# Transposing the attention probabilities of the first pair of heads with VectorE and DMAs in place of TensorE

## The chip, the cores and the metric

The kernel runs on one core of one Trainium2 chip. The core has five engines that run their own instruction streams in order: TensorE (PE in the profile; its weight loads are the row PEld), VectorE (DVE), ScalarE (ACT), GpSimd (POOL) and SyncE (SP), which here only issues DMAs. They meet by semaphores. The metric is the device time of one execution in microseconds (us). Three runs of the kernel before took 1125.55, 1126.14 and 1126.27 us; the median, 1126.14 us, is the time before. Everything is float32.

## The reference

Three layers are applied in turn to x, which is 4 batches x 256 tokens x 512: a layer of gated experts, causal attention with 32 heads, and the experts again. Each takes a layernorm of x as its input and adds to x.

```python
def _L0_attn_ref(hidden_states, wq, wkv, wo):
    q = jnp.einsum('bsd,de->bse', hidden_states, wq).reshape(B, S, H, DQ)
    kv = jnp.einsum('bsd,de->bse', hidden_states, wkv)
    k = kv[..., :H * DN].reshape(B, S, H, DN)
    v = kv[..., H * DN:H * (DN + DV)].reshape(B, S, H, DV)
    scores = jnp.einsum('bqhd,bkhd->bhqk', q[..., :DN], k) * scale
    scores = jnp.where(causal[None, None], scores, NEG_INF)
    probs = jax.nn.softmax(scores, axis=-1)
    attn = jnp.einsum('bhqk,bkhd->bqhd', probs, v).reshape(B, S, H * DV)
    return jnp.einsum('bse,ed->bsd', attn, wo)
...
x = x + 0.5 * _L0_ffn_ref(_layernorm(x, axis=-1), L0_ffn_A, L0_ffn_B, L0_ffn_Wr)
x = x + _L0_attn_ref(_layernorm(x, axis=-1), L0_attn_wq, L0_attn_wkv, L0_attn_wo)
x = x + 0.5 * _L0_ffn_ref(_layernorm(x, axis=-1), L0_ffn_A, L0_ffn_B, L0_ffn_Wr)
```

In the attention H is 32 heads, B 4 batches, S 256 tokens and DN = DV = 128. Of the 256 x 256 probabilities of a head and a batch only the causal part is computed: for the first 128 queries 128 keys, for the other 128 queries 256 keys. That is a tile of 128 partitions (queries) by 384 columns. To multiply it with the values, TensorE needs it with the keys on the partitions, so it has to be transposed in three blocks of 128 x 128.

## The kernel before, in words

**Pairs and units.** The heads are worked off in 16 pairs (NG = 16, index p). A pair has eight units, one for each head and batch (`units`, in the order head, then batch). A unit passes through `probs` (L1170): two kinds of score matmuls into one PSUM tile `ps` (L1178, L1179, 0.65 us of TensorE), the masked and scaled copy with the row minimum on VectorE (L1187, two parts), the exponential with the row sum on ScalarE (L1199, two parts), the reciprocal of the sums on VectorE (L1208), and then the division by the sum and the transposition, for which there are two ways.

- The classic way (`by_dma` false): ScalarE multiplies in place (L1212, two parts); later `turn` (L1236) has TensorE transpose the three blocks into PSUM (L1241, tile `ptp`), and ScalarE copies them to `pT` (L1245).
- The other way: ScalarE writes the multiplied probabilities to a PSUM tile `pn` in a permuted order (L1217, two parts), VectorE transposes it in blocks of 32 x 32 back into `s` (L1223, one instruction of 128 x 384), four DMAs on SP's queue bring the blocks to the tile `moved` in DRAM (L1226, 48 KB each), and one more brings `moved` to `pT` (L1232, 192 KB). TensorE has no part in it.

`probs` is a generator: each `yield` ends a piece, and `take(made, n)` issues the next n pieces. `attend` (L1247) then multiplies `pT` with the values (L1255, L1262, tile `pa`) and has ScalarE copy the result to `attn` (L1269). `pT` has two buffers, `s` and `moved` three, and the PSUM pool of `pn`, `ptp` and `pa` two.

**Which units take which way.** `classic(number)` says it: before the change the first eight units (pair 0) and the last ten are classic, the 110 between go the other way. In the middle pairs the products of a unit come 17.5 us of written time after its scores (`PRODUCT`), about three units later, and the DMA to `pT` is issued 10.8 us after them (`BACK`).

**What else runs.** Beside the units TensorE computes the queries and keys of the next pair (`make_qk`, tiles `pqk_a` to `pqk_e`, L730) and the values (`make_v`, tiles `pv_a` to `pv_e`, L829). Each stage takes seven products by Strassen's scheme; VectorE adds each product from PSUM to the results (L747 for `qk`, L854 for `vbuf`), ScalarE copies some (L754, L779, L860, L884), and GpSimd forms sums of weights (L611) and a few sums of results (L781, L886). A later product of a stage goes into the PSUM bank of an earlier one, so it waits until that one was read. The pool of these banks has five.

**What sets the order.** In pair 0 only TensorE's order is written out: `FIRST_UNITS` has one string for each unit, in which f, g, q and v take the next product of a stream of queries and keys or of values, t is a `turn` and b an `attend`, both of the unit before. The orders of the other engines and of SP's queue in pair 0 are made by a planner, which goes by the program's order and by costs that it assumes. From pair 1 on all five orders are written out, by a clock of assumed costs: `later(time, what, ...)` puts an event (`turn_at`, `attend_at`, `take`) at a time, and the products of queries, keys and values fill the rest (`goes_on`). The last pieces of pair 0, the `turn` and the `attend` of unit 7, are such events in pair 1.

Of the kernel before, what the change touches and what calls it, by code (L numbers as in the profile page):

```python
# [22 lines left out]
NG = H // HG  # L23
# [10 lines left out]
def macaron_kernel(  # L34
# [173 lines left out]
    def take(steps, n):  # L208
        for _ in range(n):
            next(steps, None)  # L210
# [421 lines left out]
    def begin_qk(p):  # L632

        weights["qk", p] = two_levels(
            qkpool,
            7,
            f"wqk_{p}",
            lambda k, n: [view[:, 2 * k : 2 * k + 2, p * HG + n, 0:DN] for view in (wq_v, wk_v)],
        )
# [530 lines left out]
    def probs(h, b, by_dma=True):  # L1170


        n = f"{h}_{b}"
        p, j = divmod(h, HG)
        half, a = divmod(b, 2)
        qT, kT = (qks[p][:, BLOCK[half][j], i, a * S : (a + 1) * S] for i in range(2))
        ps = ps_s.tile([P, 512], F32, tag="s", name=f"ps_{n}")
        nc.tensor.matmul(ps[:, 0:P], lhsT=qT[:, 0:P], rhs=kT[:, 0:P], start=True, stop=True)  # L1178
        nc.tensor.matmul(ps[:, P : 3 * P], lhsT=qT[:, P : 2 * P], rhs=kT, start=True, stop=True)  # L1179

        s = work.tile([P, 3 * P], F32, tag="s", name=f"s_{n}", bufs=3)
        least = small.tile([P, 2], F32, tag="least", name=f"least_{n}")
        den = small.tile([P, 2], F32, tag="aden", name=f"aden_{n}")
        rden = small.tile([P, 2], F32, tag="arden", name=f"arden_{n}")
        parts = (slice(0, P), slice(P, 3 * P))
        for i, cols in enumerate(parts):
            nc.vector.tensor_tensor_reduce(  # L1187
                out=s[:, cols],
                in0=ps[:, cols],
                in1=mask_f[:, cols],  # L1190
                scale=-SCALE,
                scalar=-TAKEN,
                op0=ALU.add,
                op1=ALU.min,
                accum_out=least[:, i : i + 1],
            )
        yield
        for i, cols in enumerate(parts):
            nc.scalar.activation(  # L1199
                s[:, cols],  # L1200
                s[:, cols],
                AF.Exp,
                bias=least[:, i : i + 1],
                scale=-1.0,
                accum_out=den[:, i : i + 1],
            )
        yield
        nc.vector.reciprocal(rden, den)  # L1208
        yield
        if not by_dma:  # L1210
            for i, cols in enumerate(parts):
                nc.scalar.mul(s[:, cols], s[:, cols], rden[:, i : i + 1])  # L1212
            pTs[h, b] = s
            return
        pn = ps_t.tile([P, 4, 3, 32], F32, tag="pt", name=f"pn_{n}")
        for i, cols in enumerate(parts):
            nc.scalar.mul(  # L1217
                pn[:, :, i : 2 * i + 1, :].rearrange("p k t c -> p t k c"),
                s[:, cols].rearrange("p (t k c) -> p t k c", k=4, c=32),
                rden[:, i : i + 1],  # L1220
            )
        yield
        nc.vector.transpose(s, pn.rearrange("p k t c -> p (k t c)"))  # L1223
        moved = turning.tile([P, 4, 96], F32, tag="moved", name=f"moved_{n}")
        for q in range(4):
            nc.sync.dma_start(  # L1226
                moved[:, q].rearrange("(k r) x -> r k x", r=32),
                s[32 * q : 32 * q + 32].rearrange("r (k x) -> r k x", k=4),
            )
        yield  # L1230
        pT = pTs[h, b] = work.tile([P, 4, 3, 32], F32, tag="pT", name=f"pT_{n}")
        nc.sync.dma_start(pT.rearrange("p q t c -> p (q t c)"), moved.rearrange("p q x -> p (q x)"))  # L1232
# [3 lines left out]
    def turn(h, b):  # L1236

        s = pTs[h, b]
        pt = ps_t.tile([P, 3, 4, 32], F32, tag="pt", name=f"ptp_{h}_{b}")
        for i in range(3):  # L1240
            nc.tensor.transpose(  # L1241
                pt[:, i].rearrange("p q c -> p (q c)"), s[:, i * P : (i + 1) * P], ident
            )
        pT = pTs[h, b] = work.tile([P, 4, 3, 32], F32, tag="pT", name=f"pT_{h}_{b}")
        nc.scalar.copy(pT.rearrange("p q t c -> p t q c"), pt)  # L1245
# [101 lines left out]
    units = [(h, b) for h in range(H) for b in range(B)]  # L1347
# [31 lines left out]
    def later(time, what, *of):  # L1379
        heapq.heappush(events, (time, len(events) + 1000 * len(order), what, of))  # L1380
        order.append(None)
# [18 lines left out]

    def classic(number):

        return number < 8 or number >= 8 * NG - 10


    EXP, PART, MUL, TURN, BACK, PRODUCT = 2.1, 3.5, 4.3, 6.0, 10.8, 17.5
# [56 lines left out]
    for p in range(NG):  # L1463
        last = p == NG - 1
        streams = {"q": make_qk(p + 1), "v": make_v(p), "f": first_qk, "g": first_v}
        if p == NG - 2:
            streams_o = out_products()
        if p == 0:
            for unit in range(HG * B):
                made = probs(*units[unit], False)  # L1470
                for _ in made:
                    pass
                for k in FIRST_UNITS[unit]:
                    if k in "tb":
                        if unit:
                            (turn if k == "t" else attend)(*units[unit - 1])
                    else:
                        take(streams[k], 1)
            for k in "fgqv":
                take(streams[k], 100)  # L1480
            written_out.close()
            written_out.enter_context(tc.manual_schedule(engines=ENGINES))
            rights[0][0]()
            later(1.0, turn_at, *units[7])
            later(2.2, attend_at, *units[7])
            continue
        if last:

            xscope.close()
            streaming = ExitStack()  # L1490
            stream["pool"] = streaming.enter_context(
                tc.tile_pool(name="stream", bufs=3, reuse_waits="tile")
            )
            streams["o"] = streams_o
            outer["rest"]()
            outer["load"](1)
            parts = [[("o", 0.44)] * n for n in (6, 6, 6, 5, 5, 5, 6, 6)]
        else:
            steps = merged(p)
            share = sum(cost for _, cost in steps) / 8  # L1500
            parts, t = [[] for _ in range(8)], 0.0
            for step in steps:
                parts[min(7, int((t + 0.5 * step[1]) / share))].append(step)
                t += step[1]
        for unit in range(HG * B):
            if unit == 2:
                lefts[p - 1] = left_sums_of(p - 1)

            def transfers(p=p, unit=unit):

                if p < NG - 2:
                    if unit == min(Q_LOADS):
                        begin_qk(p + 2)
                    for m in Q_LOADS.get(unit, ()):
                        weights["qk", p + 2][1](m)
                k = p // 2 + 1
                if p % 2 == 0 and 2 * k < NG:
                    if unit == min(V_LOADS):
                        begin_v(k)
                        v_by[k] = v_stages(k)  # L1520
                    for m in V_LOADS.get(unit, ()):
                        weights["v", k][1](m)
                for back in (1, 2):
                    if p - back >= 0 and not (p == NG - 1 and back == 1):
                        stores = LEFT_STORES[2 if p - back == NG - 3 else (p - back + 1) % 2].get(unit + 8 * (back - 1), ())
                        for parts in stores:
                            lefts[p - back][1](parts)
                if p == NG - 1:
                    last_transfers(unit)
                    return  # L1530
                if unit == 3:
                    rights[p - 1][2]()
                if unit == (3 if p == NG - 2 else 7):
                    rights[p][0]()
                if p == NG - 2:
                    if unit in (5, 6):
                        take(streams_o, 1)

            if p == NG - 1 and unit == 3:
                for one in lefts[p - 1][0]:  # L1540
                    one()
            written(p, unit, parts[unit], streams, transfers)
        for k in "qv":
            take(streams[k], 100)
# [87 lines left out]
```

## Time and profile before

One profiled execution took 1124.15 us, 1.99 us less than the median of the runs; its span (first to last instruction) is 1122.3 us, and 1.85 us lie around it. The rows used here:

| what | value |
|---|---|
| median of three runs | 1126.14 us (1125.55 to 1126.27) |
| profiled execution, span | 1124.15 us, 1122.3 us |
| TensorE, granted clock | 1.00 |
| stage of the change: scores of unit 0 to scores of unit 8 | 148.1 to 212.1 us of the span |
| first scores of units 1 to 7 | 152.7, 167.4, 175.6, 180.3, 188.3, 198.8, 207.3 us |
| products of units 0 to 7 | 159.5, 171.9, 178.3, 184.2, 193.2, 203.2, 210.6, 215.5 us |
| three transposes on TensorE (L1241) | 0.33 us from their start to the next matmul |
| copy of the transposed blocks (L1245) | 0.48 us |
| transposition on VectorE (L1223) | 0.577 us |

Times of single instructions are given as start and duration in us, counted from the start of the span. Matmuls overlap: an instruction's duration is longer than the time until the next one starts, and that time is what it costs TensorE. "Idle before" names the instruction that ended the wait, as the program that makes the profile infers it from semaphores. The row PEld counts the weight loads that each matmul needs.

### The profile page before, as it was taken

What the parts mean: (1) busy time and instruction counts of PE and PEld (TensorE: products, weight loads), DVE (VectorE), ACT (ScalarE), POOL (GpSimd) and SP (SyncE); (2) the same over time, 40 slices, a digit from 0 to 9 for tenths busy, and PEclk for the clock granted to TensorE, in tenths of its full rate; (3) what the DMA queues carried; (4) which work ended last, traced back from release to release, by engine and by line L of the source; (5) the groups of instructions that cost most, each with busy time, mean ns of one, the idle gap of its engine ahead of it and who ended that gap; (6) DMA issues with size and microseconds to landing.
All of it is one profiled execution on the core that took longest, in us unless ns stands there. A gap on an engine that the chain in (4) does not pass through costs nothing.

```text
span 1122.3 us, 21075 instructions
## 1 busy us (share of the span) xinstructions
PE 1110.7 (99%) x6834; PEld 977.4 (87%) x6834; DVE 807.3 (72%) x2234; ACT 441.9 (39%) x1328; POOL 626.5 (56%) x870
## 2 busy tenths in 40 slices
PE   9999999999999999999999999999999999999998
PEld 6666888899999999999999998999899999995767
DVE  5554677778778778778778778868778977865432
ACT  4453424444544544544544544544452000107310
POOL 4814487737887887887888788878532000002110
PEclk9999999999999999999999999999999999999999
DMA  9201020156756746746756756655799998750001
GB/s 332 86 1 38 29 67 16 31 145 197 203 138 195 210 136 193 207 136 192 203 152 174 210 144 183 190 166 161 205 311 321 335 348 264 243 180 1 19 19 38
DMA packets 198013, 180.06 MB, mean 160 GB/s; under 512 B 73488, under 2 KB 161296, under 8 KB 197648
## 3 DMA queue, kind: packets, MB, share of 16 engines
q1 hardware_dynamic: 197904, 178.72, 52.5%
q8 instruction: 55, 0.90, 0.3%
q14 instruction: 54, 0.44, 0.1%
HBM read 112.98 MB, written 65.67 MB: 159 GB/s over the span
## 4 chain that ended last, share of the span: by engine, by line
PE 90%; DMA 3%; DVE 2%; POOL 2%; SPq 1%; ACT 1%; issue 1%; POOLq 0%; DVEq 0%
PE po_M L1154 15%; PE po_f L422 9%; PE pqk_c L730 8%; PE ph_f L354 8%; PE pqk_b L730 8%; PE pqk_d L730 7%; PE pa L1255 5%; PE pv_c L829 4%; PE ps L1179 4%; PE pqk_a L730 3%; PE pv_b L829 3%; PE pa L1262 2%; PE ps L1178 2%; PE pv_d L829 2%; PE pv_e L829 2%; PE pv_a L829 2%
## 5 line engine op out<-in xcount | busy, mean ns | idle before, releaser
L384 POOL TENSOR_TENSOR hg_f<-hg_f,gate_f 128x512 f32<-128x512 f32 x32 | 33.5, 1059 | 259.5 <-ACT gate_f L309 151.1
L1154 PE MATMUL po_M<-or_M,ol_M 128*128 128x128 f32 x1456 | 164.7, 275 | 0.0
L1154 PEld LDWEIGHTS po_M<-or_M,ol_M 128*128 128x128 f32 x1456 | 163.7, 192 | 0.1
L611 POOL TENSOR_TENSOR wqk_M<-wqk_M 128x128 f32<-128x128 f32 x320 | 141.7, 458 | 12.1
L747 DVE TENSOR_TENSOR qk<-qk,pqk_d 128x512 f32<-128x512 f32 x210 | 116.6, 561 | 18.9 <-PE pqk_d L730 13.1
L611 POOL TENSOR_TENSOR wqk_M<-wqk_M,wqk_M 128x512 f32<-128x512 f32 (+1 forms) x64 | 107.2, 1683 | 38.7 <-DMA wqk_M<-in_wkv 23.0
L1199 ACT ACTIVATE s<-s,least 128x128 f32<-128x128 f32 (+1 forms) x256 | 114.3, 450 | 21.1 <-DVE least L1187 20.9
L1217 ACT ACTIVATE pn<-s,arden 128x128 f32<-128x128 f32 x220 | 93.7, 426 | 54.4 <-DVE arden L1208 50.7
L730 PE MATMUL pqk_c<-xop,wqk_M 128*128 128x256 f32 x448 | 111.3, 380 | 0.1
L730 PE MATMUL pqk_d<-xop,wqk_M 128*128 128x256 f32 x420 | 106.8, 381 | 1.1 <-DVE qk L747 1.1
L730 PE MATMUL pqk_b<-xop,wqk_M 128*128 128x256 f32 x420 | 104.0, 380 | 0.0
L747 DVE TENSOR_TENSOR qk<-qk,pqk_c 128x256 f32<-128x256 f32 (+1 forms) x112 | 59.7, 533 | 52.2 <-PE pqk_c L730 50.9
L1269 ACT COPY attn<-pa 128x256 f32<-128x256 f32 x128 | 47.4, 371 | 124.4 <-PE pa L1262 121.7
L1054 DVE TENSOR_TENSOR ol_M<-ol_M 128x512 f32<-128x512 f32 x104 | 75.1, 722 | 23.0 <-DMA ol_M<-left 22.6
L747 DVE TENSOR_TENSOR qk<-qk,pqk_b 128x512 f32<-128x512 f32 x105 | 71.7, 683 | 26.7 <-PE pqk_b L730 25.1
L730 PEld LDWEIGHTS pqk_c<-xop,wqk_M 128*128 128x128 f32 x448 | 78.7, 191 | 8.4 <-ACT qk L779 1.2
L1187 DVE CUSTOM_DVE_ANT_0 s<-ps,mask 128x128 f32<-128x128 f32 (+1 forms) x256 | 80.8, 353 | 3.8 <-PE ps L1179 2.6
L730 PEld LDWEIGHTS pqk_d<-xop,wqk_M 128*128 128x128 f32 x420 | 74.1, 191 | 9.9 <-DVE qk L747 2.9
L1255 PE MATMUL pa<-pT,vbuf 128*128 128x256 f32 x256 | 77.5, 384 | 3.4 <-DMA pT<-moved 2.5
L730 PEld LDWEIGHTS pqk_b<-xop,wqk_M 128*128 128x128 f32 x420 | 74.4, 191 | 7.2
L781 POOL TENSOR_TENSOR qk<-qk 128x256 f32<-128x256 f32 x64 | 46.6, 731 | 54.6 <-DVE qk L747 54.0
L1179 PE MATMUL ps<-qk 128*128 128x256 f32 x256 | 76.5, 380 | 0.0
(186 smaller groups left out, 2389.7 us busy)
## 6 DMA issues: line engine op xcount, KB each, us to landing
ol_M<-left SPq DMA_DIRECT2D x52, 512.0 KB, 5.8
moved<-s SPq DMA_DIRECT2D x440, 48.0 KB, 1.7
pT<-moved SPq DMA_DIRECT2D x110, 192.0 KB, 2.7
wv_M<-in_wkv SPq DMA_DIRECT2D x64, 128.0 KB, 2.6
wqk_M<-in_wq SPq DMA_DIRECT2D x64, 128.0 KB, 2.3
wqk_M<-in_wkv SPq DMA_DIRECT2D x64, 128.0 KB, 2.5
wo<-in_wo SPq DMA_DIRECT2D x16, 512.0 KB, 4.6
left<-attn SPq DMA_DIRECT2D x16, 512.0 KB, 3.3
```

What stands on the lines that cost most here:

```text
L354: nc.tensor.matmul(ps, lhsT=left[m][:, c, :], rhs=a_right[m][:, c, :], start=first and c == 0, stop=c == 1, skip_group_check=True,)
L422: nc.tensor.matmul(ps[:, 0:256], lhsT=left[m][:, c, :], rhs=b_right[m][:, c, :], start=first and c == 0, stop=c == 3, skip_group_check=True,)
L611: return nc.gpsimd.tensor_tensor(to, a, b, ALU.subtract)
L730: nc.tensor.matmul(ps[:, i * S : (i + 1) * S], lhsT=right[m][n], rhs=xop[OUTER[m]][:, INNER[n]], start=first and i == 0, stop=True, skip_g ...
L747: nc.vector.tensor_tensor(to, of, ps, ALU.add)
L829: nc.tensor.matmul(ps[:, i * S + t * P : i * S + (t + 1) * P], lhsT=xop[OUTER[m]][:, INNER[n], t * P : (t + 1) * P], rhs=right[m][n], star ...
L1154: nc.tensor.matmul(banks[at // 2][:, cols : cols + P], lhsT=lhsT, rhs=rhs, start=k % 4 == 0 and g == 0 and at % 2 == 0 and t == 0, stop=Tr ...
L1179: nc.tensor.matmul(ps[:, P : 3 * P], lhsT=qT[:, P : 2 * P], rhs=kT, start=True, stop=True)
L1187: nc.vector.tensor_tensor_reduce(out=s[:, cols], in0=ps[:, cols], in1=mask_f[:, cols], scale=-SCALE, scalar=-TAKEN, op0=ALU.add, op1=ALU.m ...
L1199: nc.scalar.activation(s[:, cols], s[:, cols], AF.Exp, bias=least[:, i : i + 1], scale=-1.0, accum_out=den[:, i : i + 1],)
L1217: nc.scalar.mul(pn[:, :, i : 2 * i + 1, :].rearrange("p k t c -> p t k c"), s[:, cols].rearrange("p (t k c) -> p t k c", k=4, c=32), rden[ ...
L1255: nc.tensor.matmul(po[:, 0 : 2 * P], lhsT=v_of(p, j, 2 * b), rhs=of[:, 0:2], start=True, stop=False,)
```

## The change

Of pair 0 only unit 0 stays classic; units 1 to 7 go the other way. Their pieces up to the four DMAs to `moved` are issued at the start of the unit (`take(made[unit], 5)`), the DMA from `moved` to `pT` at the b of the next unit. For units 1 to 7 the three transposes on TensorE, the copy from PSUM and the multiplication in place go; a multiplication into PSUM, a transposition on VectorE and five DMAs come. The products move: unit 0's stay in unit 1; those of units 1 to 4 come at the b of units 4 to 7, three units behind their scores; those of units 5, 6 and 7 become events of pair 1 at 2.0, 7.5 and 13.0 us, and the last DMA of unit 7 one at 2.8 us. In pair 1 three products stand where a turn and a product stood.

```diff
     def classic(number):
-        return number < 8 or number >= 8 * NG - 10
+        return number < 1 or number >= 8 * NG - 10
...
         if p == 0:
+            made = {}
             for unit in range(HG * B):
-                made = probs(*units[unit], False)
-                for _ in made:
-                    pass
+                made[unit] = probs(*units[unit], not classic(unit))
+                take(made[unit], 5)
                 for k in FIRST_UNITS[unit]:
-                    if k in "tb":
-                        if unit:
-                            (turn if k == "t" else attend)(*units[unit - 1])
+                    if k == "t":
+                        if unit and classic(unit - 1):
+                            turn(*units[unit - 1])
+                    elif k == "b":
+                        if classic(unit - 1):
+                            attend(*units[unit - 1])
+                        if unit > 2 and not classic(unit - 3):
+                            attend(*units[unit - 3])
+                        if unit and not classic(unit - 1):
+                            take(made[unit - 1], 1)
                     else:
                         take(streams[k], 1)
...
             rights[0][0]()
-            later(1.0, turn_at, *units[7])
-            later(2.2, attend_at, *units[7])
+            for unit in range(5, 8):
+                later(2.0 + 5.5 * (unit - 5), attend_at, *units[unit])
+            later(2.8, take, made[7], 1)
             continue
```

## The prediction

> **What bounds the kernel now.** I read the page's shares first, then the busy times of the stretches around the change, then the timeline of each engine there, last SP's queue and the tiles of the two ways.
>
> ```profile
> PE 1110.7 (99%) x6834; PEld 977.4 (87%) x6834; DVE 807.3 (72%) x2234; ACT 441.9 (39%) x1328; POOL 626.5 (56%) x870
> ```
>
> TensorE is busy nearly throughout, so each TensorE instruction that goes should shorten the time, unless something else takes its place. Whether it does is read stretch by stretch (length, then each engine's busy time, clock, DMA share).
>
> ```profile
> 164.60:176.40 11.80, 11.43 (x77) 10.18 (x76) 11.56 (x26) 2.99 (x9) 11.06 (x21) 1.00 0.10 24
> 176.40:188.30 11.90, 11.41 (x70) 10.35 (x69) 6.67 (x22) 6.38 (x21) 11.74 (x20) 1.00 0.08 22
> 188.30:203.50 15.20, 15.20 (x83) 13.38 (x83) 9.68 (x25) 6.38 (x21) 8.45 (x13) 1.00 0.14 37
> 203.50:212.10 8.60, 8.33 (x45) 6.58 (x44) 7.01 (x17) 3.51 (x11) 7.77 (x16) 1.00 0.11 30
> ```
>
> From 164.6 to 176.4 us VectorE (11.56 of 11.80) is fuller than TensorE (11.43). There VectorE is the bound; elsewhere TensorE is. The timeline shows both sides:
>
> ```profile
> 168.09 0.49 PE L1241 MATMUL ptp<-ident,s 128*128 128x128 f32 x3
> 168.42 0.60 PE L730 MATMUL pqk_d<-xop,wqk_M 128*128 128x256 f32 x2
> ...
> 170.71 0.70 PE L730 MATMUL pqk_d<-xop,wqk_M 128*128 128x256 f32 x2 [0.37 <-DVE qk L747]
> ...
> 171.85 0.60 PE L1255 MATMUL pa<-pT,vbuf 128*128 128x256 f32 x2
> ...
> 173.62 0.42 DVE L747 TENSOR_TENSOR qk<-qk,pqk_e 128x256 f32<-128x256 f32 x1
> ```
>
> Three transposes cost TensorE 168.42 - 168.09 = 0.33 us. At 170.71 it waited for VectorE's read of an earlier product in the same bank, and VectorE went on without a gap until the reads of stage e began at 173.62.
>
> **The change part by part.** The sum is made against the profiled execution's 1124.15 us (span 1122.3 and 1.85 around it); it goes over to the median of the runs, 1126.14, unchanged.
>
> *Removed from TensorE.* 7 turns x 0.326 us (153.35 to 153.68, 168.09 to 168.42 and so on) = -2.28 us. With them go 7 copies of 0.48 us on ScalarE (39% busy) and 7 multiplications in place (2 x 0.40); those were beside other work, worth nothing by themselves.
>
> *Units 2 and 3, where VectorE is the bound.* Two gaps in TensorE's own work go: the turn of unit 1 at 168.09 (0.33) and, moved to unit 4, the product of unit 1 at 171.85 (0.66 until 172.51). The wait at 170.71 ends when VectorE has read the fifth product (169.97 + 0.68 = 170.65), whatever TensorE did before; so the 0.33 become wait. Stage e then starts at 171.85 in place of 172.51, but its third product goes into the bank of the first, which VectorE reads from 173.62 on (ready 0.42 later, 174.04). Without more on VectorE that product starts at 174.10 (before: 174.27), and the scores of unit 3 at 175.41 (before: 175.58). So of 0.99 us of work gone only 0.17 are won: +0.82. In addition unit 2's transposition falls here: its multiplication ended on ScalarE at 171.36 + 0.80 = 172.16, and VectorE's backlog lasts until 176. It takes 0.577, some 0.5 of them before the next one starts (in pair 1: 226.17 to 226.67). It stands early in the program, so I expect the planner to put it into the backlog: +0.48. Together +1.30. Ends: only the turn lost, +0.33, and all of it, +1.30; I take +1.30, since each row of the timeline points there.
>
> *Unit 4.* TensorE idled 0.49 us before 183.25. The profile names GpSimd's weight sums, but those of the weights in use were done; the third product goes into the first one's bank, and ScalarE's read of that was late:
>
> ```profile
> 181.48 0.48 ACT L1245 COPY pT<-ptp 128x384 f32<-128x384 f32 x1 [1.82 <-PE ptp L1241]
> 181.86 0.40 ACT L1199 ACTIVATE s<-s,least 128x128 f32<-128x128 f32 x1
> ...
> 182.75 0.36 ACT L754 COPY qk<-pqk_a 128x256 f32<-128x256 f32 x1
> ```
>
> The copy at 181.48 goes. If the exponentials still come before the read, the read ends 2.1 us after the scores in place of 2.15, so of the 0.33 us turn here only 0.05 are won: +0.28. If the planner puts the read first, since its product is ready first, the wait goes too: -0.49. I take 0, between the two.
>
> *Units 5 to 7.* TensorE has no idle time from 188.3 to 203.5, so the turns there count in full. At 206.79 it waited 0.23 us for VectorE, which is full from 204.53 on; unit 6's transposition comes ready at 201.70 + 0.9 = 202.6, just ahead. VectorE has gaps of 0.29 and 0.33 us before that: +0.2, between 0 and 0.5.
>
> *The other five transpositions on VectorE.* Units 1, 3, 4, 5 and 7 come ready at about 156.5, 179.5, 184.1, 192.0 and 211.0 us, in gaps of 0.42, 0.67, 1.99, 0.62 and 0.67 us: 0 each. If that cover is gone, up to 0.5 each, +2.5.
>
> *Products moved into pair 1.* Three products (3 x 0.65) for a turn and a product: what pair 0 loses pair 1 gets, so the work adds up to zero. TensorE shows no idle time from 212.1 to 230, where the hand-written order runs. Pair 1's early units then look like those of the later pairs, with one product a unit, where these rows show how little TensorE waits for the DMAs:
>
> ```profile
> L1223 DVE STREAM_TRANSPOSE s<-pn x110: 574/577/580, 220.7 to 804.7; 128x384 f32<-128x384 f32 x110
> ...
> PE pa L1255 <- DMA pT<-moved: 2.5, 6, 0.6
> ```
>
> *SP and the DMAs.* 7 x (four issues in 1.76 us, one of 0.34) = 14.7 us of SP's time, against waits on weights' buffers of 14 us at a time:
>
> ```profile
> 180.01 0.47 SPq L608 DMA_DIRECT2D wqk_M<-in_wkv  x1
> 194.54 0.37 SPq L608 DMA_DIRECT2D wqk_M<-in_wq  x1
> ```
>
> A unit's way is 1.5 us to the minimum, 1 exponential, 1 reciprocal and multiplication, 0.6 transposition, 1.8 issue, 2.0 landing, 2.7 for the last DMA: 10.6 us after its scores, some 12 where VectorE is behind. The products come 31.5, 25.8, 27.6, 30.3 us after the scores of units 1 to 4, some 18 or more for 5 to 7. So 6 us or more are spare: 0. The last DMA of a unit also waits for the product two units before (two buffers of `pT`), and the weight loads at 194.54 and 202.57 may stand behind it. If they start 2 us later, GpSimd sums later; its sums end at 214.5, and the stage that needs the last of them starts at 233: hidden. With that cover gone rival C below is the upper end, +3.
>
> Sum: -2.28 + 1.30 + 0 + 0.2 + 0 = -0.8 us. That gives 1123.35 for the profiled execution and 1125.3 for the median.
>
> [...] By the rows a block of 128 x 128 costs TensorE 0.109 us (0.326 / 3) and VectorE 0.19 (0.577 / 3): 21 blocks free 2.28 and add 4.0 us. [...]
>
> **The rivals.** (A) The full gain. The -2.28 us count but for the one turn at 168.09 (+0.33), and unit 4's wait goes too (-0.49): -2.4, so 1123.7. For it: TensorE is at 99%, and the transposition may come after the backlog. Against it: 11.56 of 11.80 us on VectorE.
>
> (B) Slower, by waits at the head of VectorE's queue. Each unit gets one more hand-over from ScalarE to VectorE, whose place in pair 0 the planner sets by assumed costs. If ScalarE is late, VectorE stands at the transposition while reads of products queue behind it, and TensorE waits for the banks. The kernel before shows such waits at the hand-over before it:
>
> ```profile
> DVE arden L1208 <- ACT s L1199: 1.2, 2, 1.1
> ...
> DVE vbuf L854 <- ACT s L1199: 0.6, 1, 0.6
> DVE qk L747 <- ACT s L1199: 0.6, 1, 0.6
> ```
>
> These are 0.6 us each, the longest 1.1. If each of the seven units waits 0.6 us and TensorE with it, the sum is -0.8 + 7 x 0.6 = +3.4: 1129.5. It turns the sign from 0.12 us a unit on, and can be told from no change from 0.44 on. Against it: the waits shown lie where VectorE has time to spare and cost TensorE nothing, and only two stretches are full on VectorE.
>
> (C) SP's queue: a unit's DMAs stand behind the load that waits from 180.48 to 194.54. Unit 3's, ready at 180, then start at 196.5 and bring `pT` by 196.5 + 1.8 + 2.0 + 2.7 = 203.0, and its product stands at about 201.5; 1.5 us, or 3 if a second unit fares so: 1126.8 to 1128.3. Against it: the planner orders by when things come ready.
>
> **How the numbers follow.** About 0.2% (2.25 us) is what a measurement of this kernel can tell from no change. Forecast 0.52, A 0.18, B 0.2, C 0.1. The forecast lies within 0.2%; its own range is 1123.7 to 1127.2 (the ends of units 2 to 6, and half of the five transpositions). A is split around 1123.9; with the waits of 0.37 and 0.23 us gone too it reaches 1123.1. B counts as slower for the most part, C for half. So faster 0.15, same 0.59, slower 0.26. The range that holds 8 in 10 goes from A's far end to B's price: 1123.0 to 1129.5.
>
> **What would show it.** L1241 falls from 54 to 33 and L1223 rises from 110 to 117. TensorE's waits for VectorE in stages d and e of pair 0 grow by about 1 us; unit 2's transposition stands in VectorE's backlog; the first scores of unit 8 come 1.8 us earlier (0.8, and two products of 0.65 moved behind them, less the turn of 0.33 that stood behind them before), and pair 2 starts 0.8 us earlier. The wait before pair 0's next stage a tells what became of unit 4's read. It would be wrong if TensorE waited for `pT<-moved`, if VectorE waited for ScalarE's `pn`, or if the weight loads of SP slid by several microseconds.

## The result

The changed kernel is slower, by little. Twenty runs of each kernel gave medians of 1126.26 us (1123.69 to 1128.43) and, for the kernel before, 1125.16 us (1123.05 to 1126.82). The ratio is 1.0014 with a 95% interval of 1.0008 to 1.0021: +0.9 to +2.4 us. The forecast of 1125.3 us, 0.8 us below the median it was made against, has the time inside its range and the sign wrong.

### The profile page after: what moved, and what is told of

The parts are those of the page before. It is cut to its first block, busy times and chain, and to the rows that moved or that the text cites. A ratio compares the mean times of both kernels' runs of the same rounds, so it can differ in the third digit from the quotient of the medians.

```text
span 1125.0 us, 21111 instructions
## 1 busy us (share of the span) xinstructions
PE 1109.1 (99%) x6813; PEld 975.7 (87%) x6813; DVE 811.0 (72%) x2241; ACT 439.4 (39%) x1321; POOL 626.4 (56%) x870
## 4 chain that ended last, share of the span: by engine, by line
PE 85%; DMA 4%; POOL 4%; DVE 3%; issue 1%; ACT 1%; SPq 1%; DVEq 0%; POOLq 0%
PE po_M L1154 13%; PE po_f L422 8%; PE ph_f L354 8%; PE pqk_b L730 8%; PE pqk_c L730 8%; PE pqk_d L730 7%; PE pa L1255 4%; PE pv_c L829 4%; PE ps L1179 4%; PE pv_b L829 4%; PE pqk_a L730 3%; PE pa L1262 2%; PE ps L1178 2%; PE pv_d L829 2%; POOL wqk_M L611 2%; PE pv_e L829 2%
## 5 line engine op out<-in xcount | busy, mean ns | idle before, releaser
L1217 ACT ACTIVATE pn<-s,arden 128x128 f32<-128x128 f32 x234 | 99.7, 426 | 54.0 <-DVE arden L1208 50.0
```

What stands on the lines that cost most here:

```text
L1217: nc.scalar.mul(pn[:, :, i : 2 * i + 1, :].rearrange("p k t c -> p t k c"), s[:, cols].rearrange("p (t k c) -> p t k c", k=4, c=32), rden[ ...
```

## The profile after

The first part of the page of the changed kernel, and the rows of the tiles of the two ways:

```profile
PE 1109.1 (99%) x6813; PEld 975.7 (87%) x6813; DVE 811.0 (72%) x2241; ACT 439.4 (39%) x1321; POOL 626.4 (56%) x870
```

```profile
L1241 PE MATMUL ptp<-ident,s x33: 272/273/273, 154.4 to 853.7; 128*128 128x128 f32 x33
L1223 DVE STREAM_TRANSPOSE s<-pn x117: 574/577/584, 157.0 to 806.3; 128x384 f32<-128x384 f32 x117
```

The work moved as the change says: 54 transposes on TensorE became 33, 110 on VectorE became 117, and TensorE's busy time fell by 1.6 us. The span of this execution is 1125.0 us, against 1122.3. A span alone doesn't show where the 2.7 us came from, since two executions of one program differ by as much (the twenty runs of the kernel before by up to 3.8): 1.01 us of them lie ahead of unit 0, in the first layer, where both programs have the same instructions in the same order on every engine (one wait of TensorE was 1.4 us in place of 0.5). They have it again from the seventh unit of pair 1 on, and there the difference wanders: the reciprocal of a unit comes 1.89 us later at 239 us of the span before, 0.25 us at 730, and the last additions 2.5 us at 1119. So I read the stretch of the change by a measure that leaves the rest out. The **lag** of a unit is the start of its first score matmul (L1178), counted from that of unit 0, less the same in the kernel before. From unit 11 (the fourth of pair 1) on all moved products are done, and the lag there is what the change cost in its stretch.

| unit | 1 | 2 | 3 | 4 | 5 | 6 | 7 | 9 | 11 |
|---|---|---|---|---|---|---|---|---|---|
| changed kernel, lag in us | +0.01 | +1.64 | +2.04 | +1.05 | +0.34 | +0.01 | +0.29 | -0.43 | +0.88 |

The 0.88 us at unit 11 lie at the lower end of the runs' +0.9 to +2.4 and contradict -0.8. The largest step is between units 1 and 2, 1.63 us, where I had put zero. VectorE's timeline there, and the one line of TensorE's that goes with it (start, duration, instruction, in brackets the idle time before it and what ended it):

```profile
155.13 0.08 DVE L1187 DVE_READ_ACCUMULATOR2_ANT least<- 128x1 f32 x1
155.92 0.17 DVE L1208 RECIPROCAL arden<-aden 128x2 f32<-128x2 f32 x1 [0.71 <-ACT s L1199]
157.03 0.58 DVE L1223 STREAM_TRANSPOSE s<-pn 128x384 f32<-128x384 f32 x1 [0.95 <-ACT pn L1217]
157.54 1.25 DVE L854 TENSOR_TENSOR vbuf<-vbuf,pv_c 128x512 f32<-128x512 f32 x2
```

```profile
158.24 1.16 PE L829 MATMUL pv_c<-wv_M,xop 128*128 128x128 f32 x8 [1.60 <-DVE vbuf L854]
```

Unit 1's transposition stands in VectorE's queue ahead of two reads of `pv_c` that could have gone first. VectorE stood idle 0.71 us for the exponentials and 0.95 us for the multiplication into PSUM, and the product of `pv_c` that goes into the bank of the first of these reads waited 1.60 us. That VectorE waits for `pn` is what the prediction had named as a sign that it would be wrong. In the kernel before, one of these reads started at 154.84, between the minimum and the reciprocal, and no wait of TensorE followed:

```profile
154.84 0.69 DVE L854 TENSOR_TENSOR vbuf<-vbuf,pv_c 128x512 f32<-128x512 f32 x1 [0.65 <-ACT s L1199]
155.45 0.16 DVE L1208 RECIPROCAL arden<-aden 128x2 f32<-128x2 f32 x1
```

The stretches that answer to those of the prediction (length, busy time of TensorE, its weight loads, VectorE, ScalarE, GpSimd, clock, DMA share, GB/s; here cut at the units' new places):

```profile
157.00:159.00 2.00, 0.76 (x6) 0.76 (x7) 1.75 (x3) 0.41 (x2) 1.97 (x4) 1.00 0.14 29
167.30:178.60 11.30, 10.34 (x63) 8.49 (x63) 11.30 (x26) 2.15 (x7) 10.83 (x21) 1.00 0.16 39
178.60:189.70 11.10, 10.96 (x66) 9.90 (x66) 7.77 (x26) 5.25 (x18) 10.94 (x19) 1.00 0.33 81
189.70:204.00 14.30, 14.30 (x76) 12.63 (x75) 10.27 (x27) 5.74 (x18) 8.24 (x10) 1.00 0.32 80
204.00:210.00 6.00, 5.12 (x27) 3.87 (x26) 5.05 (x11) 0.93 (x3) 5.92 (x12) 1.00 0.43 109
```

The first holds the wait at unit 1. In the second, stages d and e, VectorE has not one idle moment (11.30 of 11.30), and TensorE loses 0.96 us. In the last, stage d of the next queries and keys, TensorE loses 0.88. In the third it is idle 0.14 us, behind unit 4's transposition; the fourth is whole.

## The experiments

Theory H: what costs is the place of an instruction in VectorE's queue. The planner put a transposition ahead of reads that TensorE needs; on the chip ScalarE was not done yet, and the reads queued behind it. (That by the planner's assumed costs ScalarE would have been done is likely, but its costs are in no trace; what the runs test is the place.) Against it stood: a cost of every transposition (S), the transposition's own time (W), something in unit 1 itself (U). Each kernel was also timed against the kernel before, on the same chip; intervals are 95%.

| kernel | unit 2 | 3 | 4 | 5 | 6 | 7 | 11 | ratio to before |
|---|---|---|---|---|---|---|---|---|
| changed kernel | +1.64 | +2.04 | +1.05 | +0.34 | +0.01 | +0.29 | +0.88 | 1.0014 (1.0008 to 1.0021) |
| only unit 1 changed | +1.64 | +1.57 | +1.57 | +2.22 | +2.23 | +2.22 | +2.59 | 1.0029 (1.0018 to 1.0040) |
| unit 1's transposition held | +0.14 | +0.54 | -0.45 | -1.17 | -1.49 | -1.23 | -0.64 | 1.0003 (0.9994 to 1.0012) |
| units 1's and 2's held | +0.14 | +0.07 | -0.92 | -1.63 | -1.96 | -2.29 | -1.70 | 0.9995 (0.9986 to 1.0004) |
| unit 1 classic | 0.00 | +5.22 | +4.24 | +3.04 | +2.71 | +2.97 | +3.57 | 1.0023 (1.0014 to 1.0033) |
| unit 1's held, its product in unit 2 | +0.14 | +0.53 | -0.45 | -1.65 | -1.98 | -2.31 | -1.72 | 0.9988 (0.9979 to 0.9996) |
| all mends | 0.00 | 0.00 | -0.98 | -2.18 | -2.51 | -2.84 | -2.24 | 0.9985 (0.9976 to 0.9994) |
| unit 1 classic, unit 2's held | 0.00 | +0.88 | -0.10 | -1.30 | -1.63 | -1.96 | -1.37 | 0.9992 (0.9984 to 1.0000) |
| unit 1's held, GpSimd pinned | +0.14 | +0.54 | -0.45 | -1.16 | -1.49 | -1.82 | -1.23 | 0.9992 (0.9984 to 1.0001) |

The lags resolve more than the ratios: the ratio tells the version with all mends from the changed kernel, but not the one with unit 1's transposition held. In all rows but that of unit 1 classic the ratio is also higher than the lag at unit 11 would make it, by 0.3 to 1.1 us. What comes to it behind unit 11 stays open.

To hold or pin an instruction means that its piece is issued later in the program and `keep_in_program_order` keeps the planner from moving it forward again.

### Only unit 1 goes the new way

```diff
-        return number < 1 or number >= 8 * NG - 10
+        return number != 1 and number < 8 or number >= 8 * NG - 10
...
-            for unit in range(5, 8):
-                later(2.0 + 5.5 * (unit - 5), attend_at, *units[unit])
-            later(2.8, take, made[7], 1)
+            later(1.0, turn_at, *units[7])
+            later(2.2, attend_at, *units[7])
```

> Of pair 0 only unit 1 goes by VectorE and DMAs; its product still comes three units later, the other seven units are classic. The lag of a unit is the start of its first score matmul, counted from that of unit 0, minus the same in the kernel before. VectorE's order at unit 1 is that of the changed kernel: minimum, reciprocal, transposition, then three reads of pv_c. Theory H (VectorE stands at unit 1's transposition for ScalarE while reads of pv_c queue behind it): TensorE waits about 1.6 us for a read of pv_c, the lag of unit 2 is +1.6 us; unit 3 +1.4 (the turn and the product that go from unit 2 are swallowed by VectorE's backlog), and with the product back in unit 4 unit 11 lags +2.1: slower than before by about 2 us although only one unit is changed. Rival S (the 0.88 us of the changed kernel are a cost of each transposition, spread over seven units): a lag of about +0.1 us at unit 2 and at unit 11.

Lag +1.64 at unit 2 and +2.59 at unit 11, ratio 1.0029. The waits repeat to the hundredth: 0.71 and 0.95 us on VectorE, 1.60 on TensorE. By its lag one unit alone costs more than all seven together, since the other six give back some of it. S falls. From unit 7 to unit 9 came 0.38 us more that I had not expected and did not follow up.

### Unit 1's transposition behind the reads of pv_c

```diff
-        nc.vector.transpose(s, pn.rearrange("p k t c -> p (k t c)"))
+        turned = nc.vector.transpose(s, pn.rearrange("p k t c -> p (k t c)"))
+        if pinned:
+            tc.keep_in_program_order(turned)
...
+    HELD = {1: 4}
...
-                made[unit] = probs(*units[unit], not classic(unit))
-                take(made[unit], 5)
-                for k in FIRST_UNITS[unit]:
+                made[unit] = probs(*units[unit], not classic(unit), unit in HELD)
+                take(made[unit], 4 if unit in HELD else 5)
+                for i, k in enumerate(FIRST_UNITS[unit]):
+                    if i == HELD.get(unit):
+                        take(made[unit], 1)
```

> The changed kernel, with unit 1's transposition traced after the three last products of pv_c and pinned behind their reads on VectorE. Theory H: the reads no longer wait for ScalarE's multiplication; the reciprocal still stands before them and waits some 0.7 us for the exponentials, so unit 2 lags +0.35 us in place of +1.6, and unit 11 some -0.4 in place of +0.88. Rival W (the transposition's own time on VectorE and the added work there are the cost, wherever it stands): unit 2 still lags +1.1 us or more, unit 11 +0.4 or more.

Unit 2 lags +0.14, unit 11 -0.64. The transposition is the same and as long; in VectorE's order it is the only instruction that moved, and ScalarE's order is the same. VectorE's timeline:

```profile
155.68 0.17 DVE L1208 RECIPROCAL arden<-aden 128x2 f32<-128x2 f32 x1 [0.71 <-ACT s L1199]
155.76 1.36 DVE L854 TENSOR_TENSOR vbuf<-vbuf,pv_c 128x512 f32<-128x512 f32 x2
157.69 0.42 DVE L854 TENSOR_TENSOR vbuf<-vbuf,pv_c 128x256 f32<-128x256 f32 x1 [0.57 <-PE pv_c L829]
158.03 0.57 DVE L1223 STREAM_TRANSPOSE s<-pn 128x384 f32<-128x384 f32 x1
```

The reciprocal still holds VectorE up for 0.71 us, which costs TensorE 0.14; the transposition starts without any wait. So of unit 2's lag of 1.64 us 0.14 belong to the reciprocal and 1.50 to the transposition's place: its wait of 0.95 and some 0.5 of its own time. H holds, W falls.

### Unit 2's transposition out of the backlog too

```diff
-    HELD = {1: 4}
+    HELD = {1: 4, 2: 14}
```

> As the run before, and unit 2's transposition pinned behind unit 2's last product, out of VectorE's backlog. Theory H with the prediction's step for units 2 and 3 (a transposition in the backlog costs its 0.5 us, out of it nothing): unit 3 lags 0.5 us less than in the run before, about +0.2 in place of +0.75, and unit 11 about -0.9. Rival: the backlog only shifts, since the transposition is still to be done before unit 3's scores are read: unit 3 as in the run before, unit 11 -0.4.

Unit 3 lags +0.07 in place of +0.54: 0.47 us, against 0.5 expected. Unit 7 gains a further 0.6 us that nobody had put there, which the last experiment takes up. Unit 11 is at -1.70, 0.8 better than expected: 0.6 for that reason, and 0.2 because the run before stood at -0.64 in place of the -0.4 reckoned with.

### Unit 1 stays classic

```diff
-        return number < 1 or number >= 8 * NG - 10
+        return number < 2 or number >= 8 * NG - 10
```

> Units 0 and 1 classic, units 2 to 7 by VectorE and DMAs. The planner now puts unit 2's reciprocal and transposition straight behind its minimum, before the fifth to seventh reads of pqk_d. Theory H (the place on VectorE decides, not the unit): VectorE stands there about 1 us for the exponentials and 0.9 us for the multiplication, in the stretch where it is full, so unit 2 lags 0, unit 3 about +2.3, and unit 11 about +0.5 us. Rival U (the cost belongs to unit 1, because its products are those of pv_c): unit 2 lags 0, unit 3 about +0.3, unit 11 about -1.1 us, the fastest of these kernels.

U falls: with unit 1 out of it, unit 2 does the same in its place, and worse. Unit 3 lags +5.22, more than twice the +2.3 that H gave. VectorE's and TensorE's lines:

```profile
170.99 0.17 DVE L1208 RECIPROCAL arden<-aden 128x2 f32<-128x2 f32 x1 [0.71 <-ACT s L1199]
172.10 0.58 DVE L1223 STREAM_TRANSPOSE s<-pn 128x384 f32<-128x384 f32 x1 [0.95 <-ACT pn L1217]
172.61 0.65 DVE L747 TENSOR_TENSOR qk<-qk,pqk_d 128x512 f32<-128x512 f32 x1
173.31 1.22 PE L730 MATMUL pqk_d<-xop,wqk_M 128*128 128x256 f32 x2 [2.75 <-DVE qk L747]
```

The wait is 2.75 us, 2.38 more than the 0.37 of the kernel before, as H gave. What comes on top is in the granted clock (the number behind GpSimd's count) of the stretches around it:

```profile
166.00:170.50 4.50, 4.50 (x32) 4.01 (x30) 4.28 (x11) 0.53 (x3) 4.23 (x6) 1.00 0.02 5
170.50:173.30 2.80, 0.06 (x1) 0.00 (x0) 1.36 (x4) 1.71 (x5) 2.75 (x7) 0.89 0.00 0
173.30:176.50 3.20, 3.19 (x11) 2.81 (x12) 2.95 (x5) 0.00 (x0) 3.04 (x7) 0.50 0.34 67
176.50:179.70 3.20, 3.20 (x13) 2.83 (x13) 1.26 (x3) 0.37 (x1) 3.12 (x4) 0.53 0.24 61
179.70:183.00 3.30, 3.30 (x23) 3.04 (x22) 2.80 (x10) 0.79 (x3) 3.30 (x7) 1.00 0.00 0
```

After the wait TensorE ran at half its clock almost to the end of these 6.4 us (0.50 and 0.53; an estimate from the means of 0.89 and 0.53, if the clock was either 1.00 or 0.50, puts the half clock from 172.7 to 179.5) and did 24 matmuls where the next 3.3 us held 23. The same matmuls, from the one that waited to the third product of stage e, took 6.40 us here (173.31 to 179.71) and 3.56 in the kernel before (170.71 to 174.27): 2.84 us lost. With the 2.38 of the wait that is the 5.22 seen.

### The same with unit 2's transposition held

```diff
+    HELD = {2: 14}
...
-        return number < 1 or number >= 8 * NG - 10
+        return number < 2 or number >= 8 * NG - 10
```

> Units 0 and 1 classic as in the run that was slower by 0.23%, but unit 2's transposition pinned out of VectorE's backlog; its reciprocal still stands straight behind the minimum. In that run TensorE waited 2.75 us at once and the granted clock was 0.50 to 0.53 for the 6.4 us after it; unit 3 lagged +5.22. Theory C (2.3 us of that lag are the wait at the head of VectorE's queue, some 3 us are the halved clock that the long wait brought on): with only the reciprocal's 0.7 us at the head the wait stays under 1.5 us, the clock at 1.00, and unit 3 lags +0.7 to +0.9; unit 11 lies at -0.9 to -1.5. Rival (the clock is halved by something else in this kernel): the clock falls again at the same place, and unit 3 lags +3 or more.

Unit 3 lags +0.88, unit 11 -1.37. TensorE's longest wait for VectorE (total, number, longest) and the clock in the same stretch as above:

```profile
PE pqk_d L730 <- DVE qk L747: 1.5, 2, 1.2
```

```profile
173.30:176.50 3.20, 3.20 (x23) 3.00 (x23) 3.20 (x8) 0.37 (x1) 3.04 (x7) 1.00 0.02 5
```

The clock stays at 1.00. One instruction of 0.58 us, moved in VectorE's queue, is worth 4.3 us at unit 3: 1.5 of wait and 2.84 of halved clock.

### Unit 1's product back in unit 2

```diff
-                        if unit > 2 and not classic(unit - 3):
+                        if unit == 2:
+                            take(made[1], 1)
+                            attend(*units[1])
+                        elif unit > 2 and unit != 4 and not classic(unit - 3):
                             attend(*units[unit - 3])
-                        if unit and not classic(unit - 1):
+                        if unit > 2 and not classic(unit - 1):
                             take(made[unit - 1], 1)
```

> The changed kernel with unit 1's transposition behind the reads of pv_c, and in addition unit 1's product back at the b of unit 2, where the kernel before has it, its last DMA just ahead. Lags as in the runs before; with unit 1's transposition held alone they were +0.14 at unit 2, +0.54 at unit 3, -0.45 at unit 4, -1.17 at unit 5 and -0.64 at unit 11. Theory F (units 2 and 3 are timed by VectorE's backlog, so a product there costs TensorE nothing): unit 3 stays at about +0.54, and from unit 5 on, where the product no longer stands, everything is 0.66 us earlier: unit 5 -1.83, unit 11 -1.30. Rival (a product costs its 0.66 us wherever it stands): unit 3 +1.2, unit 5 and unit 11 unchanged at -1.17 and -0.64.

Unit 3 stays at +0.53, unit 5 falls from -1.17 to -1.65: 0.48 of the 0.66 us. So in the stretch where VectorE is the bound the product cost TensorE nothing; moved out of it, as the change does, it cost 0.48 us where it went. The 0.18 that are missing are a balance at unit 4. A new wait for ScalarE's read of `pqk_a` (0.2 us of idle time) costs 0.54 us from start to start of the products, and a wait for VectorE behind unit 4's transposition, 0.38 by the same count, goes. Unit 11 is at -1.72, lower than expected, because unit 7's 0.6 us are gone here too.

### All mends

Unit 1's reciprocal pinned behind one read of `pv_c` and its transposition behind three, unit 2's reciprocal pinned where the planner had it and its transposition behind the backlog, unit 1's product in unit 2:

```diff
-        nc.vector.reciprocal(rden, den)
+        divided = nc.vector.reciprocal(rden, den)
+        if pinned:
+            tc.keep_in_program_order(divided)
...
+    HELD = {1: (2, 2, 4), 2: (14,)}
...
+                held = HELD.get(unit, ())
+                made[unit] = probs(*units[unit], not classic(unit), unit in HELD)
+                take(made[unit], 5 - len(held))
+                for i, k in enumerate(FIRST_UNITS[unit]):
+                    take(made[unit], held.count(i))
```

> All mends together: unit 1's reciprocal pinned behind one read of pv_c and its transposition behind three, unit 2's transposition out of the backlog, unit 1's product in unit 2. If the theories H and F hold and add up: unit 2 lags 0, unit 3 about 0, unit 5 about -2.3, unit 11 -2.4 with TensorE's own saving of 2.28 nearly whole: 0.2% faster than the kernel before. If they do not add up (the backlog of VectorE takes back what the product gives): unit 11 no better than with the two transpositions held, -1.70.

Units 2 and 3 lag 0.00, unit 11 -2.24, near the 2.28 us that seven turns cost. That is a balance: the first turn, in the stretch that VectorE times, is not won (unit 3 lags 0.00), and from unit 4 to 5 the lag falls by 1.20 where a turn and a product, 0.99, went. The ratio is 0.9985 (0.9976 to 0.9994), a median of 1122.65 us against 1123.94 of the kernel before on the same chip. By these ratios this version is faster than both kernels.

### GpSimd's order

```diff
-            sum_all(("qk", p + 1), p == 0)
+            sum_all(("qk", p + 1), True)
```

added to the kernel with unit 1's transposition held.

> The changed kernel with unit 1's transposition behind the reads of pv_c, and the first sum of the next weights pinned behind the sums of queries and keys on GpSimd, so that only four weight sums stand between these; VectorE's order is as without the pin. With unit 1's transposition held alone units 6, 7 and 11 lagged -1.49, -1.23 and -0.64, and VectorE waited 0.51 us for a GpSimd sum of qk in between. Theory P (the planner's new order on GpSimd makes unit 6's stall): unit 7 about -1.8, unit 11 about -1.2. Rival T (unit 6's transposition ahead of VectorE's full stretch makes it, as the prediction had it): unit 7 -1.23 and unit 11 -0.64 as before.

Unit 7 lags -1.82, unit 11 -1.23: as theory P had it, which put the 0.6 us of unit 7 down to GpSimd's order. VectorE's order is unchanged, with unit 6's transposition in the same place, so the transposition is not the cause. Without the pin VectorE waited there for a GpSimd sum of `qk` that the planner had put behind six weight sums; with it two stand there. First GpSimd in the kernel with unit 1's transposition held, then VectorE and TensorE in the changed kernel, which has the same six:

```profile
201.30 2.65 POOL L611 TENSOR_TENSOR wqk_M<-wqk_M 128x128 f32<-128x128 f32 x6
203.90 0.73 POOL L781 TENSOR_TENSOR qk<-qk 128x256 f32<-128x256 f32 x1
```

```profile
206.42 0.69 DVE L747 TENSOR_TENSOR qk<-qk,pqk_d 128x512 f32<-128x512 f32 x1 [0.52 <-POOL qk L781]
```

```profile
207.16 0.70 PE L730 MATMUL pqk_d<-xop,wqk_M 128*128 128x256 f32 x2 [0.65 <-DVE qk L747]
```

In the kernel with units 1's and 2's held, where the 0.6 us went too, GpSimd's order also differs, without a pin. The change touches no instruction of GpSimd. That the planner put its sums elsewhere because its own clock for GpSimd's inputs had moved is my reading of it; the runs show only that the order changed and what that cost.

## Why the prediction was wrong, point by point

- **Removed from TensorE, -2.28:** right as the time of seven turns: where TensorE is the bound the lag falls by 0.33 with each (units 5 to 6 of the changed kernel). That the version with all mends ends near it, at -2.24, is a balance, as said there.
- **The other five transpositions, 0 each: the step that failed.** Units 3, 5 and 7 were right, unit 4 cost 0.3 us, and unit 1 cost 1.63 us, three times the upper end of 0.5. I had compared the time when unit 1's transposition comes ready (156.5) with VectorE's gap beside it (0.42 us) and taken the gap for its cover. But VectorE works in order: the first read behind the transposition started 1.62 us after the reciprocal (155.92 and 157.54), and with the transposition held 0.08 us after it (155.68 and 155.76). What counts is which instruction stands at the head of its queue, and the transposition, put there too early, cost the wait for its input besides its own time. The bound of 0.5 covers the transposition's own time; it left out that wait (0.95 us) and the reciprocal's place (0.14).
- **Rival B named the mechanism and priced it wrongly:** 0.6 us for each of seven units. The runs show 1.66 us of waits on VectorE at one unit and 1.60 on TensorE, 0.3 at unit 4, and no such wait of TensorE at the others. VectorE's waits for ScalarE in the stretch (microseconds, number, longest) came to 2.4 us before (1.2 + 0.6 + 0.6, in the prediction) and to 3.6 in the changed kernel; the hand-over to the transposition is new, and the others shrank:

```profile
DVE s L1223 <- ACT pn L1217: 2.4, 3, 1.3
...
DVE arden L1208 <- ACT s L1199: 1.2, 3, 0.7
```

  The longest, 1.3 us, is at unit 4. It lay where hardly a read was ready, but the transposition's own time behind it put off a read of `pqk_a`, and the product that goes into that bank started 0.30 us late (187.46; 0.44 us after 186.71, where the matmuls ahead of it started, would be 187.15). In the kernel with unit 1's product in unit 2 the same read stands ahead of the transposition, and the product is not late:

```profile
186.42 0.58 DVE L1223 STREAM_TRANSPOSE s<-pn 128x384 f32<-128x384 f32 x1 [1.32 <-ACT pn L1217]
186.93 0.71 DVE L747 TENSOR_TENSOR qk<-qk,pqk_a 128x256 f32<-128x256 f32 x2
187.46 0.67 PE L730 MATMUL pqk_a<-xop,wqk_M 128*128 128x256 f32 x2
```

- **Units 2 and 3, +1.30:** right, +1.39 (a lag that rose by 0.40 with 0.99 us of work gone). Its two parts were shown apart: the transposition in the backlog 0.47 us (0.48 forecast), and 0.92 (0.82) for the turn and the product whose time became waits. That the product was free there the run with it back in unit 2 shows: unit 3 starts no later (+0.53 for +0.54).
- **Unit 4, 0 between -0.49 and +0.28:** -0.38. The lag fell by 0.71, of which 0.33 are the turn. The 0.38 are again a balance: the wait before 183.25 went, 0.73 us from start to start of the products (0.49 counts its idle time alone), and the one behind unit 4's transposition came, 0.38 by the same count. ScalarE did the read first, as the lower end supposed:

```profile
183.65 0.37 ACT L754 COPY qk<-pqk_a 128x256 f32<-128x256 f32 x1 [1.73 <-PE pqk_a L730]
183.92 0.41 ACT L1199 ACTIVATE s<-s,least 128x128 f32<-128x128 f32 x1
```

  The kernel with unit 1 alone changed still has the old order and the wait of 0.5 us at that place, and there the profile names ScalarE's read as its end: my reading of the row that named GpSimd was right.
- **Units 5 to 7, +0.2:** +0.61, just past its end of 0.5, and for another reason than I gave: GpSimd's order, not the transposition.
- **SP and the DMAs, 0:** right. No product of the stretch waited for a DMA in the changed kernel. So rival C fell; A did not come. Unit 8's scores came 2.13 us earlier, counted from unit 0, where 1.8 had been named as a sign; that did not tell the kernels apart, since in the changed kernel products of stage e that stood ahead of these scores stand behind them.
- **The sum:** -2.28 + 1.63 + 1.39 - 0.38 + 0.61 = +0.97, against +0.88 measured; the 0.09 left over were not followed up. The difference to the forecast, 1.7 us, is unit 1's 1.63; that the errors of unit 4 (-0.38) and unit 6 (+0.41) cancel is luck.

I had argued that the planner would put unit 2's transposition early because it stands early in the program, and did not ask the same of unit 1, where the consequence was worse.

## What to carry to other kernels

On an engine that works in order, an added instruction has two prices: its own time, and the wait for its input at the head of the queue (at unit 1 some 0.5 and 0.95 us). The second is paid by whatever stands behind it, and free time on the engine was no cover for it: beside a gap of 0.42 us unit 2 came 1.63 us later. Where a planner sets the order by assumed costs, look for the hand-over from another engine (here ScalarE) and pin the receiving instruction behind the reads that the busiest engine needs. And before moving work off the bounding engine, check stretch by stretch whether it is the bound there: here a product in a stretch that VectorE times was free (unit 3 at +0.53 with it, +0.54 without), and moving it away made it cost 0.48 us.

## What the runs showed of the hardware

- In the kernel with unit 1 classic a wait of 2.75 us of TensorE (170.56 to 173.31) brought its granted clock from 1.00 to 0.50. By the estimate from the means above that was at 172.7, 2.1 us into the wait, and the clock was 1.00 again at 179.5, after 6.2 us of steady matmuls. The wait of 1.60 us at unit 1 of the changed kernel left it at 1.00 (157.0 to 159.0), as did one of 1.2 in the kernel with unit 1 classic and unit 2's transposition held. So a wait that was 1.15 us longer cost 2.84 more. The stretches are those of one execution; of the ten runs of this kernel seven had a mean granted clock of 0.997 or 0.998 and three of 1.0. Waits between 1.60 and 2.75 us were not tried.
- Two programs that differ in the path of the six units behind it (the changed kernel and the one with unit 1 alone changed) gave the same waits to 0.01 us at unit 1 (0.71, 0.95 and 1.60 us), while the twenty runs of the kernel before spread over 3.8 us and those of the changed kernel over 4.7. For changes of 0.1% the start of one instruction relative to an earlier one tells more than the span.
